# A two-layer graph network on one core: layer 1's values in one run, the transposes of x an iteration ahead, the output bias beside the scores

## The chip, the core and the metric

The kernel runs on one core of a Trainium2 chip. The core has engines with a queue each, which run side by side [...]: TensorE (PE, matmuls; PEld is its loading of weights), VectorE (DVE), ScalarE (ACT), GpSimd (POOL), and SyncE, whose queue (SPq) issues the DMAs. The metric is device time in microseconds (us) from the first to the last instruction; the median of three runs counts.

## The reference

64 graphs of 256 nodes with 512 features go through two layers. Everything is fp32.

```python
# layer 0: graph attention, 8 heads of 64
feats = einsum('bnf,hfu->bhnu', X, W)
dense = leaky_relu(e_self[..., :, None] + e_neigh[..., None, :], 0.2)
att = softmax(dense + NEG_BIG * (1.0 - A))
x = layernorm(x + relu(einsum('bhij,bhju->bhiu', att, feats) + b))
# layer 1: attention plus adjacency and exp(-distance), both from the same matrix
qkv = x @ W_qkv
attn = 0.33 * softmax(q k^T * scale) + 0.33 * adj + 0.33 * exp(-adj)
x = layernorm(x + (attn v) @ W_out + b_out)
```

## The kernel before

**Tiling.** A graph's 256 nodes are two tiles of 128 rows. A large product (features of layer 0, q and k, v) is cut 2 by 2 by 2 and done with seven block products instead of eight (`seven`, L289). They are named p1 to p7 and are called here f-products (`pf_p`, features of layer 0), q-products (`pq_p`) and v-products (`pv_p`). Each adds up in one of three PSUM banks: p1, then p6, p7 and p4 in the bank "chain"; p2 in "alone"; p5, then p3 in "pair". A product of the chain is copied out by ACT (L309) before the next one may add to that bank, since the copy is of the partial sum. DVE then adds a bank to what was copied (L312, steps 11, 22, 12); step 22 reads "pair" after p5 and before p3, so p3 must wait for it.

**Transposes.** The seven products need x transposed, and sums of its quarters. x is loaded in blocks (`load`, L125, tile `xb`), turned by one DVE instruction (L121, tile `xT`), and four DVE subtractions make the sums (`left_factors`, L273, tile `xC`). The same is done with layer 0's output (`hb`, `hT`, `hC`). `xT` and `hT` share two buffers in turn.

**Three graphs at once.** An iteration b of the main loop (L1299) works on attention of layer 0 for graph b, on the projections and scores of layer 1 for graph b-1, on the attention of layer 1 for graph b-2, and on the features of layer 0 for graph b+1. It has two parts. `attention0_beside_projections1` (L1132): q-products, the weights of layer 0 (`weights`, L632, tiles `pT`, four buffers for eight heads), their product with the features (`product` of attend0, L648), v-products, norm of layer 0, f-products. `attention1_beside_projections0` (L1212): values of layer 1 (L903), scores (L798), output projection (L991), the softmax's sums, `hT`. 

**What sets the order.** Each engine's order is written out by hand: `do` (L1030) calls one step, and `in_order` (L86) ties every instruction to the one before it on its engine, so no engine overtakes within its own queue. An instruction that waits holds everything behind it on that engine. The values of layer 0 come in two halves of four heads; "product g, t" is half g for node tile t. Half 1 reuses the four `pT` buffers of half 0.

**The long transfer.** Layer 0's row factors go from PE (`pr`) through ACT and DVE to HBM and back to all partitions (`gs`, then `gb`, 1 MB; L482 to 487). DVE's `nd` (L528) waits for `gb`, then ACT makes `ccol` (L535), then DVE makes `pT` (L637).

**Norm of layer 0.** DVE's `end` (L681) adds x and the row sums, POOL makes the mean (L346), ACT squares two tiles and reads two accumulators (L351), POOL makes the factors, ACT scales (L367). Then layer 0's output goes to HBM and comes back in blocks as `hb`.

Of the kernel before, what the change touches and what calls it, by code (L numbers as in the profile page):

```python
# [8 lines left out]
FT = mybir.dt.float32  # L9
# [8 lines left out]
def kernel(  # L18
# [30 lines left out]
    P = 128  # L49
    NB, N, F = x.shape  # L50
    H, _, U = w0.shape
    T = N // P
    C = F // P
# [326 lines left out]
    def attention_vectors(g, step):  # L380
# [30 lines left out]
                )  # L411
        in_order()

    def proj0(b):
        xT = work.tile([P, C, N], FT, tag="xT", name=f"xT_{b}")
        if b > 1:
            xC = work.tile([P, 4, C2, P], FT, tag="xC", name=f"xC_{b}", bufs=1)

        V0[b] = work.tile([P, T, H, UX], FT, tag="v0", name=f"v0_{b}", bufs=1)
        if b > 1:  # L420
# [178 lines left out]
                    scale=V0[b][:, t, h, U : U + 1],  # L599
                )  # L600

        def transposes():
            transpose_blocks(xT, XB[b])
            if b > 1:
                left_factors(xC, xT)

        return dict(
            copied=copied,
            logits=logits,
            maxima=maxima,  # L610
            factors=factors,
            xT=transposes,
            product=product,
            add=add,
            bias=bias,
# [267 lines left out]
    def attend1(b):  # L883
# [139 lines left out]


    stages = dict(
        proj0=proj0, attend0=attend0, proj1=proj1, softmax1=softmax1, attend1=attend1
    )
    S = {}

# [8 lines left out]
    def start():  # L1038

        tiles = [slice(t, t + 1) for t in range(T)]  # L1040
        do("proj0", 0, "xT_rows")
        for g in range(2):
            for t in range(T):
                do("proj0", 0, "features", t, g)
                do("proj0", 0, "logits", t, g)
                do("proj0", 0, "copied", t, g)
            if g == 0:
                do("proj0", 0, "aT")
                load_adj(1)
                do("proj0", 0, "far")  # L1050
        attention_vectors(0, 0)
        attention_vectors(1, 0)
        do("proj0", 0, "maxima")
        attention_vectors(0, 1)
        do("proj0", 1, "xT")
        do("proj0", 0, "columns")
        do("proj0", 0, "factors")
        attention_vectors(1, 1)
        attention_vectors(0, 2)
        attention_vectors(1, 2)  # L1060
        attention_vectors(2, 0)
        attention_vectors(3, 0)
        for h in range(2):
            do("proj0", 0, "scaled", h)
            do("attend0", 0, "weights", h)
        attention_vectors(2, 1)
        attention_vectors(3, 1)
        attention_vectors(2, 2)
        attention_vectors(3, 2)
        for h in range(2, HG):  # L1070
            do("proj0", 0, "scaled", h)
            do("attend0", 0, "weights", h)
        do("proj0", 1, "features", 0, 0)
        do("proj0", 1, "features", 0, 1)
        do("attend0", 0, "product", 0, 0)
        do("attend0", 0, "product", 0, 1)
        for h in range(HG, H):
            do("proj0", 0, "scaled", h)
            do("attend0", 0, "weights", h)
        do("proj0", 1, "features", 1, 0)  # L1080
        do("attend0", 0, "product", 1, 0)
        do("attend0", 0, "product", 1, 1)
        do("proj0", 1, "features", 1, 1)
        do("attend0", 0, "norm0", 0, 0)
        do("attend0", 0, "norm0", 0, 1)
        combine_weights1(0)
        do("attend0", 0, "norm0", 1, 0)
        do("attend0", 0, "end", tiles[0])
        do("attend0", 0, "squares", tiles[0])
        do("attend0", 0, "norm0", 1, 1)  # L1090
        do("attend0", 0, "end", tiles[1])
        do("attend0", 0, "squares", tiles[1])
        do("attend0", 0, "norm", tiles[0])
        for t in range(T):
            for g in range(2):
                do("proj0", 1, "copied", t, g)
        load_rows(1)
        do("proj0", 1, "maxima")
        do("proj0", 1, "columns")
        do("proj0", 0, "shared")  # L1100
        do("proj0", 1, "aT")
        do("proj1", 0, "from_rows", 0)
        do("attend0", 0, "norm", tiles[1])
        do("proj1", 0, "qk", "p1")
        do("proj1", 0, "from_rows", 1)
        do("proj1", 0, "hC")
        do("proj1", 0, "qk", "p2")
        do("proj0", 1, "far")
        do("proj0", 1, "factors")
        combine_weights1(1)  # L1110
        combine_weights1(2)
        load(2)
        load_adj(2)
        do("proj1", 0, "qk_add", 11)
        do("proj1", 0, "qk", "p6")
        for h in range(HG):
            do("proj0", 1, "scaled", h)
            do("attend0", 1, "weights", h)
        do("proj1", 0, "qk", "p5")
        do("proj1", 0, "qk", "p7")  # L1120
        do("proj1", 0, "qk_add", 22)
        combine_weights1(3)
        for h in range(HG, H):
            do("proj0", 1, "scaled", h)
            do("attend0", 1, "weights", h)
        do("proj1", 0, "qk", "p4")
        do("proj1", 0, "qk", "p3")
        do("proj1", 0, "qk_add", 12)
        right_factors(wf_sb, wf12)
        in_order()  # L1130

    def attention0_beside_projections1(b):  # L1132


        if b > 1:
            do("attend1", b - 3, "squares")
            do("proj1", b - 1, "qk", "p1")
            do("proj1", b - 1, "qk", "p2")
            do("proj0", b, "columns")
            do("proj1", b - 1, "qk", "p6")  # L1140
            for h in range(HG):
                do("proj0", b, "scaled", h)
                do("attend0", b, "weights", h)
            do("attend1", b - 3, "store")
            do("proj1", b - 1, "qk_add", 11)
            do("proj1", b - 1, "qk", "p5")
            do("proj1", b - 1, "qk", "p7")
            do("attend1", b - 2, "residual")
            do("proj1", b - 1, "qk_add", 22)
        do("attend0", b, "product", 0, 0)  # L1150
        if b > 1:
            for h in range(HG, H):
                do("proj0", b, "scaled", h)
            do("proj1", b - 1, "qk", "p4")
        do("attend0", b, "product", 0, 1)
        do("attend1", b - 2, "weights", 0)
        if b > 1:
            for h in range(HG, H):
                do("attend0", b, "weights", h)
        do("attend0", b, "norm0", 0, 0)  # L1160
        do("attend0", b, "norm0", 0, 1)
        if b > 1:
            do("proj1", b - 1, "qk", "p3")
            do("proj1", b - 1, "qk_add", 12)
        do("proj0", b + 1, "xT")
        if b == 1:
            do("proj0", 1, "shared")
            load_rowmask()
            nc.sync.dma_start(bo_bc, b_out.partition_broadcast(P))
            nc.sync.dma_start(wo_sb, w_out.rearrange("(c p) f -> p c f", p=P))  # L1170
            in_order()
        if b + 2 < NB:
            load(b + 2)
        do("proj1", b - 1, "values", "p1")
        do("proj1", b - 1, "values", "p2")
        do("proj1", b - 1, "v_add", 11)
        do("attend0", b, "product", 1, 0)
        do("proj1", b - 1, "values", "p6")
        do("proj1", b - 1, "values", "p5")
        do("attend0", b, "product", 1, 1)  # L1180
        do("attend1", b - 2, "weights", 1)
        do("attend0", b, "norm0", 1, 0)
        do("attend0", b, "norm0", 1, 1)
        do("attend0", b, "end")
        do("proj1", b - 1, "values", "p7")
        do("proj1", b - 1, "v_add", 22)
        do("proj0", b + 1, "product", "p1")
        do("proj1", b - 1, "values", "p4")
        do("proj0", b + 1, "product", "p6")
        do("proj1", b - 1, "values", "p3")  # L1190
        do("attend0", b, "squares")
        do("attend1", b - 2, "weights", 2)
        do("proj1", b - 1, "v_add", 12)
        do("proj0", b + 1, "product", "p5")
# [17 lines left out]
    def attention1_beside_projections0(b):  # L1212


        do("attend1", b - 2, "values", 0)
        do("attend1", b - 2, "values", 1)
        do("softmax1", b - 1, "scores", 0)
        do("proj0", b + 1, "shared")
        do("softmax1", b - 1, "both", 0)
        do("softmax1", b - 1, "scores", 1)  # L1220
        do("softmax1", b - 1, "both", 1)
        do("proj0", b + 1, "bias")
        do("attend1", b - 2, "values", 2)
        do("attend1", b - 2, "values", 3)
        do("softmax1", b - 1, "scores", 2)
        do("softmax1", b - 1, "both", 2)
        do("softmax1", b - 1, "scores", 3)
        do("softmax1", b - 1, "both", 3)
        do("attend1", b - 2, "project", 0)
        do("proj0", b + 1, "rows")  # L1230
        do("proj1", b, "hT")
        do("attend1", b - 2, "project", 1)
        do("softmax1", b - 1, "sums")
        do("softmax1", b - 1, "invert")
        ps_tile([P, F], f"turn_{b}")

    def end():
# [113 lines left out]
```

## Time and profile before

| | |
|---|---|
| time, median of three | 3157.45 us (3157.37 to 3158.32) |
| busy: PE, PEld | 3032.9 us (96%), 2329.3 us (74%) |
| busy: DVE, ACT, POOL | 2628.4 us (83%), 1492.4 us (47%), 202.1 us (6%) |
| DMA | 328.20 MB, mean 104 GB/s |
| granted TensorE clock | 0.99 |
| chain that ended last | PE 53%, DVE 33%, ACT 7%, DMA 5% |

A timeline of the profile has one row for each run of equal instructions: start in us, duration in us, engine, source line, operation, output<-inputs, shape and count. What stands in brackets at its end is how long the engine was idle before it and which engine's instruction ended that. The duration of a row reaches to the end of its last instruction; the next row can begin a little earlier, because instructions of one engine overlap, so distances between starts ("pitch") are what adds up. One iteration is the distance between two equal rows: `pv_p` after its wait stands at 2022.63 us and again at 2070.74, 2118.56, 2166.38 and 2214.20, so 47.8 us (48.1 in the first of these).

### The profile page before, as it was taken

To read this page: it belongs to the slowest core of one execution; us is meant where nothing else is said; L and a number is where in the kernel's file an instruction comes from. 1 tells how busy PE (TensorE), PEld (TensorE's weight loads), DVE (VectorE), ACT (ScalarE), POOL (GpSimd) and SP (SyncE) were. 2 spreads that over 40 slices of the span, in tenths; PEclk is the share of its full clock that TensorE was granted. 3 is DMA by queue.
4 is the path that set the end of the run, shared out by engine and by line. 5 is a ranking of instruction groups with operands and counts; after the bars stand their busy time and mean duration, and the time that the engine had idled before them with its cause. 6 is when DMAs were issued, how large, how long until landed. Compare 5 with 4: busy or idle time off the path is not lost.

```text
span 3157.0 us, 64599 instructions
## 1 busy us (share of the span) xinstructions
PE 3032.9 (96%) x25526; PEld 2329.3 (74%) x25526; DVE 2628.4 (83%) x5151; ACT 1492.4 (47%) x3585; POOL 202.1 (6%) x526
## 2 busy tenths in 40 slices
PE   8899999999999999999999999999999999999998
PEld 7777777777777777777777777777777777777775
DVE  4888888888888888888888888888888888888885
ACT  2444444454454445444444544544444445445443
POOL 0000000000000000000000000000000000000000
PEclk7999999999999999999999999999999999999999
DMA  5344344344344344443444444444434434444331
GB/s 122 77 112 107 99 115 103 98 122 95 105 121 96 106 107 99 112 107 97 117 95 105 123 93 108 109 98 111 107 98 116 98 102 122 95 105 115 94 97 47
DMA packets 760611, 328.20 MB, mean 104 GB/s; under 512 B 693516, under 2 KB 694268, under 8 KB 744312
## 3 DMA queue, kind: packets, MB, share of 16 engines
q1 hardware_dynamic: 758200, 323.55, 40.6%
q8 instruction: 204, 3.34, 0.5%
q14 instruction: 95, 0.78, 0.1%
q10 hardware_dynamic: 2112, 0.52, 0.1%
HBM read 256.13 MB, written 67.61 MB: 103 GB/s over the span
## 4 chain that ended last, share of the span: by engine, by line
PE 53%; DVE 33%; ACT 7%; DMA 5%; issue 2%; SPq 0%; POOL 0%; DVEq 0%; POOLq 0%
PE po L994 13%; PE pq_p L300 9%; PE pf_p L300 9%; PE pz L804 8%; PE av L909 7%; DVE pT L637 7%; DVE p L899 5%; DVE p L892 4%; PE pv_p L300 3%; ACT v L595 3%; DVE qk L312 3%; DVE x L686 3%; DVE x L675 3%; DMA gb<-gs 2%; DVE xT L121 2%
## 5 line engine op out<-in xcount | busy, mean ns | idle before, releaser
L300 PE MATMUL pq_p<-hC,wqk_sb 128*128 128x128 f32 x4096 | 487.3, 277 | 4.2 <-ACT qk L309 4.2
L300 PEld LDWEIGHTS pq_p<-hC,wqk_sb 128*128 128x128 f32 x4096 | 469.1, 192 | 10.4 <-ACT qk L309 5.7
L994 PE MATMUL po<-wo_sb,oT 128*128 128x512 f32 x1024 | 466.3, 599 | 0.0
L637 DVE SCALAR_TENSOR_TENSOR pT<-gb,ccol,at 128x256 f32<-128x256 f32 x992 | 403.4, 479 | 17.6 <-ACT ccol L535 17.6
L300 PE MATMUL pq_p<-hT,wqk_sb 128*128 128x128 f32 x3072 | 380.9, 281 | 3.5 <-DVE hT L121 2.5
L300 PEld LDWEIGHTS pq_p<-hT,wqk_sb 128*128 128x128 f32 x3072 | 356.6, 193 | 34.3 <-DVE hC L278 23.9
L309 ACT COPY v<-pv_p 128x256 f32<-128x256 f32 x256 | 95.4, 373 | 573.5 <-PE pv_p L300 573.3
L300 PE MATMUL pv_p<-wv_sb,hC 128*128 128x256 f32 x1024 | 274.0, 400 | 95.5 <-DVE v L312 95.5
L351 ACT ACTIVATE junk<-x,nmean_l 128x512 bf16<-128x512 f32 x256 | 184.8, 722 | 342.9 <-POOL nmean_l L346 338.8
L813 ACT ACTIVATE p<-pz,hide 128x512 f32<-128x512 f32 x512 | 310.3, 689 | 59.6 <-PE pz L804 59.5
L994 PEld LDWEIGHTS po<-wo_sb,oT 128*128 128x128 f32 x1024 | 184.7, 190 | 207.5 <-issue 206.1
L899 DVE TENSOR_TENSOR p<-p,ct 128x1024 f32<-128x1024 f32 x252 | 308.7, 1225 | 8.6
L892 DVE TENSOR_TENSOR p<-p,rb 128x1024 f32<-128x1024 f32 x252 | 304.4, 1208 | 7.8 <-DMA rb<-rs 7.8
L660 PEld LDWEIGHTS av<-v,pT 128*64 128x64 f32 x8192 | 259.4, 138 | 57.5 <-issue 21.6
L660 PE MATMUL av<-v,pT 128*64 128x65 f32 x8192 | 294.5, 225 | 0.0
L300 PEld LDWEIGHTS pv_p<-wv_sb,hC 128*128 128x128 f32 x1024 | 179.3, 190 | 147.8 <-DVE v L312 121.7
L825 DVE SCALAR_TENSOR_TENSOR both<-p 128x512 f32<-128x512 f32 x256 | 176.6, 690 | 99.2 <-ACT p L813 99.1
L595 ACT ACTIVATE v<-v 128x64 f32<-128x64 f32 x1024 | 258.5, 339 | 0.0
L300 PE MATMUL pf_p<-wf_sb,xC 128*128 128x264 f32 x992 | 258.1, 394 | 0.0
L804 PE MATMUL pz<-qk 64*128 64x256 f32 x2048 | 256.2, 389 | 0.8 <-ACT p L813 0.8
L909 PE MATMUL av<-p,v 128*64 128x256 f32 x2016 | 245.4, 385 | 0.0
L804 PEld LDWEIGHTS pz<-qk 64*128 64x128 f32 x2048 | 187.1, 186 | 67.9 <-ACT p L813 26.0
(137 smaller groups left out, 3797.2 us busy)
## 6 DMA issues: line engine op xcount, KB each, us to landing
rb<-rs SPq DMA_DIRECT2D x63, 1024.0 KB, 4.7
gb<-gs SPq DMA_DIRECT2D x62, 1028.0 KB
xb<-in_x_dram SPq DMA_DIRECT2D x252, 128.0 KB, 3.7
x<-in_x_dram SPq DMA_DIRECT2D x63, 512.0 KB
hs<-x SPq DMA_DIRECT2D x63, 512.0 KB
hb<-hs SPq DMA_DIRECT2D x252, 128.0 KB, 3.5
out_dram<-x SPq DMA_DIRECT2D x63, 512.0 KB, 3.9
adj<-in_adj_dram SPq DMA_DIRECT2D x256, 64.0 KB, 4.4
```

The lines of the kernel that those rows point to most:

```text
L300: matmul(d, lhsT, rhs, start=(p in FIRST and i == 0), stop=(i == len(todo) - 1), skip_group_check=True,)
L351: nc.scalar.activation(junk, self.src[:, t, :], AF.Square, bias=self.nmean[:, t : t + 1], accum_out=self.rstd[:, t : t + 1],)
L595: nc.scalar.activation(V0[b][:, t, h, :U], V0[b][:, t, h, :U], AF.Copy, scale=V0[b][:, t, h, U : U + 1],)
L637: nc.vector.scalar_tensor_tensor(pT[h][:, j, :], GB[b][h], CCOL[b][:, j, h : h + 1], AT[b][:, j, :], op0=ALU.max, op1=ALU.mult,)
L660: matmul(av[r * half : (r + 1) * half, k, :], pT[h][:, j, i : i + half], V0[b][:, j, h, :UA], start=(j == 0), stop=(j == T - 1),)
L804: matmul(pz[:, r, j, :], QK[b][rows, g, 1, j * P : (j + 1) * P], QK[b][rows, g, 0, :], start=True, stop=True,)
L813: nc.scalar.activation(p[:, :, j, :], pz[:, :, j, :], AF.Exp, bias=hide[:, j, b : b + 1], scale=U**-0.5,)
L825: nc.vector.scalar_tensor_tensor(both[g], p[:, :, 0, :], TINY, p[:, :, 1, :], op0=ALU.add, op1=ALU.add)
L892: nc.vector.tensor_mul(p, p, REC[b][:, k : k + 2, g // 2, :] .unsqueeze(2) .to_broadcast([P, 2, T, N]),)
L899: nc.vector.tensor_add(p, p, CT[b].unsqueeze(1).to_broadcast([P, 2, T, N]))
L909: matmul(av[0][r * U : (r + 1) * U, g % 2, :], V1[b][:, j, 2 * g + r, :], PROBS[b][g][:, r, j, :], start=(j == 0), stop=(j == T - 1),)
L994: matmul(po, oT[:, c, t * P : (t + 1) * P], wo_sb[:, c, :], start=(c == 0), stop=(c == C - 1),)
```

## The change

Four moves; no instruction is added or left out.

1. **Layer 0's values in two visits.** PE did product 0,0; q p4; product 0,1; q p3; v p1, p2; product 1,0; v p6, p5; product 1,1; v p7. It now does product 0,0 and 0,1 together, q p4, q p3, product 1,0 and 1,1 together, and then v p1, p2, p6, p5, p7. DVE makes the second half's `pT` before the first `weights` of layer 1 and not after it, and `end` ahead of v's step 11 and layer 1's second `weights`.
2. **x's transposes an iteration ahead.** A new stage `turned` holds them. `xT` of graph b+2 is made in the second part of iteration b, after the bias of layer 0 and before the third `both` (L825); the four subtractions come at the end of the iteration, after `invert`. Before, both stood in the first part of iteration b+1, between q's step 12 and v's step 11.
3. **The output bias** (`residual`, L986) moves from between q's steps 11 and 22 to the scores, ahead of the projection.
4. **The norm of layer 0 ahead.** `squares` moves from after v p3 to after v p7, ahead of f p1. On ACT its two squares now stand between the copy of v p7 and the copy of f p1; before they stood after the copy of f p6.

```diff
+    def turned(b):
+        def transposes():
+            XT[b] = work.tile([P, C, N], FT, tag="xT", name=f"xT_{b}")
+            transpose_blocks(XT[b], XB[b])
+        def sums():
+            XC[b] = work.tile([P, 4, C2, P], FT, tag="xC", name=f"xC_{b}", bufs=1)
+            left_factors(XC[b], XT[b])
...
             do("proj1", b - 1, "qk", "p7")
-            do("attend1", b - 2, "residual")
             do("proj1", b - 1, "qk_add", 22)
         do("attend0", b, "product", 0, 0)
+        do("attend0", b, "product", 0, 1)
         if b > 1:
             for h in range(HG, H):
                 do("proj0", b, "scaled", h)
             do("proj1", b - 1, "qk", "p4")
-        do("attend0", b, "product", 0, 1)
-        do("attend1", b - 2, "weights", 0)
-        if b > 1:
             for h in range(HG, H):
                 do("attend0", b, "weights", h)
         do("attend0", b, "norm0", 0, 0)
         do("attend0", b, "norm0", 0, 1)
+        do("attend1", b - 2, "weights", 0)
         if b > 1:
             do("proj1", b - 1, "qk", "p3")
             do("proj1", b - 1, "qk_add", 12)
-        do("proj0", b + 1, "xT")
...
+        do("attend0", b, "product", 1, 0)
+        do("attend0", b, "product", 1, 1)
         do("proj1", b - 1, "values", "p1")
         do("proj1", b - 1, "values", "p2")
-        do("proj1", b - 1, "v_add", 11)
-        do("attend0", b, "product", 1, 0)
-        do("proj1", b - 1, "values", "p6")
-        do("proj1", b - 1, "values", "p5")
-        do("attend0", b, "product", 1, 1)
-        do("attend1", b - 2, "weights", 1)
         do("attend0", b, "norm0", 1, 0)
         do("attend0", b, "norm0", 1, 1)
         do("attend0", b, "end")
+        do("proj1", b - 1, "v_add", 11)
+        do("proj1", b - 1, "values", "p6")
+        do("proj1", b - 1, "values", "p5")
+        do("attend1", b - 2, "weights", 1)
         do("proj1", b - 1, "values", "p7")
         do("proj1", b - 1, "v_add", 22)
+        do("attend0", b, "squares")
         do("proj0", b + 1, "product", "p1")
         do("proj1", b - 1, "values", "p4")
         do("proj0", b + 1, "product", "p6")
         do("proj1", b - 1, "values", "p3")
-        do("attend0", b, "squares")
         do("attend1", b - 2, "weights", 2)
...
         do("proj0", b + 1, "bias")
+        if b + 2 < NB:
+            do("turned", b + 2, "xT")
...
         do("softmax1", b - 1, "both", 3)
+        do("attend1", b - 2, "residual")
         do("attend1", b - 2, "project", 0)
...
         do("softmax1", b - 1, "invert")
+        if b + 2 < NB:
+            do("turned", b + 2, "xC")
```

More of the change, by code (lines that the diff above doesn't have):

```diff
@@ L412, in attention_vectors @@
         in_order()
+    XT, XC = {}, {}
+    def turned(b):
[5 more added lines that the diff above has]
+            left_factors(XC[b], XT[b])
+        return dict(xT=transposes, xC=sums)
     def proj0(b):
-        xT = work.tile([P, C, N], FT, tag="xT", name=f"xT_{b}")
-        if b > 1:
-            xC = work.tile([P, 4, C2, P], FT, tag="xC", name=f"xC_{b}", bufs=1)
+        if b == 0:
+            XT[b] = work.tile([P, C, N], FT, tag="xT", name=f"xT_{b}")
+        xT, xC = XT[b], XC.get(b)
         V0[b] = work.tile([P, T, H, UX], FT, tag="v0", name=f"v0_{b}", bufs=1)
@@ L600, in scaled @@
                 )
[L602 to L605, printed above, removed]
         return dict(
@@ L611, in proj0 @@
             factors=factors,
-            xT=transposes,
             product=product,
@@ L1025 @@
     stages = dict(
-        proj0=proj0, attend0=attend0, proj1=proj1, softmax1=softmax1, attend1=attend1
+        turned=turned, proj0=proj0, attend0=attend0, proj1=proj1, softmax1=softmax1, attend1=attend1
     )
@@ L1054, in start @@
         attention_vectors(0, 1)
-        do("proj0", 1, "xT")
+        do("turned", 1, "xT")
         do("proj0", 0, "columns")
@@ L1154, in attention0_beside_projections1 @@
             do("proj1", b - 1, "qk", "p4")
-        do("attend0", b, "product", 0, 1)
-        do("attend1", b - 2, "weights", 0)
-        if b > 1:
             for h in range(HG, H):
@@ L1164, in attention0_beside_projections1 @@
             do("proj1", b - 1, "qk_add", 12)
-        do("proj0", b + 1, "xT")
-        if b == 1:
-            do("proj0", 1, "shared")
+        else:
+            do("turned", b + 1, "xT")
+            do("turned", b + 1, "xC")
+            do("proj0", b, "shared")
             load_rowmask()
```

## The prediction

> **What bounds the kernel now.** I read the page first, then the waits, then the timelines of PE, DVE and ACT over one ordinary iteration. The page has PE busy nearly all the time, so only what PE still waits for can be won.
>
> ```profile
> PE 3032.9 (96%) x25526; PEld 2329.3 (74%) x25526; DVE 2628.4 (83%) x5151; ACT 1492.4 (47%) x3585; POOL 202.1 (6%) x526
> ```
>
> The waits of PE come down to one: a v-product waits for a DVE addition, 63 times, that is once per iteration. (Columns: engine and line, whom it waited for, us in total, times, longest.)
>
> ```profile
> PEld pv_p L300 <- DVE v L312: 121.7, 63, 3.7
> PE pv_p L300 <- DVE v L312: 95.5, 63, 3.3
> ```
>
> PE's timeline shows where. The `pv_p` at 2022.63 is v p3, which stands idle until v's step 22 has read the bank "pair".
>
> ```profile
> 2017.49 1.13 PE L300 MATMUL pv_p<-wv_sb,hC 128*128 128x256 f32 x4
> 2018.46 1.05 PE L300 MATMUL pf_p<-wf_sb,xT 128*128 128x264 f32 x4
> 2019.35 1.03 PE L300 MATMUL pv_p<-wv_sb,hT 128*128 128x256 f32 x4
> 2020.21 1.05 PE L300 MATMUL pf_p<-wf_sb,xC 128*128 128x264 f32 x4
> 2022.63 1.13 PE L300 MATMUL pv_p<-wv_sb,hC 128*128 128x256 f32 x4 [1.36 <-DVE v L312]
> ...
> 2028.14 1.95 PE L909 MATMUL av<-p,v 128*64 128x256 f32 x16
> ```
>
> DVE's timeline says why. From `nd` to step 22 (2022.15) it hardly rests, and xT with xC lies in that stretch. Later, beside the scores, DVE idles several times.
>
> ```profile
> 2014.37 1.23 DVE L121 STREAM_TRANSPOSE xT<-xb 128x1024 f32<-128x1024 f32 x1
> 2015.63 0.42 DVE L276 TENSOR_TENSOR xC<-xT 128x256 f32<-128x256 f32 x1
> ...
> 2017.11 0.42 DVE L312 TENSOR_TENSOR v<-pv_p,v 128x256 f32<-128x256 f32 x1
> ...
> 2022.15 0.42 DVE L312 TENSOR_TENSOR v<-pv_p,v 128x256 f32<-128x256 f32 x1
> ...
> 2036.31 0.69 DVE L825 SCALAR_TENSOR_TENSOR both<-p 128x512 f32<-128x512 f32 x1 [0.79 <-ACT p L813]
> ...
> 2039.91 0.69 DVE L922 SCALAR_TENSOR_TENSOR x<-po,x 128x512 f32<-128x512 f32 x1 [1.75 <-PE pr L82]
> ...
> 2049.24 0.18 DVE L528 TENSOR_TENSOR nd<-v,gb 128x16 f32<-128x16 f32 x1 [1.58 <-DMA gb<-gs]
> ```
>
> ACT's timeline is where the change will bite: three copies, each right after its product, and then the two squares of layer 0's norm.
>
> ```profile
> 2018.66 0.37 ACT L309 COPY v<-pv_p 128x256 f32<-128x256 f32 x1 [2.63 <-PE pv_p L300]
> 2019.61 0.38 ACT L309 COPY v<-pf_p 128x264 f32<-128x264 f32 x1 [0.57 <-PE pf_p L300]
> ...
> 2021.31 0.38 ACT L309 COPY v<-pf_p 128x264 f32<-128x264 f32 x1 [0.52 <-PE pf_p L300]
> 2022.58 0.72 ACT L351 ACTIVATE junk<-x,nmean_l 128x512 bf16<-128x512 f32 x1 [0.89 <-POOL nmean_l L346]
> 2023.20 0.19 ACT L351 ACTIVATION_READ_ACCUMULATOR junk<-x,nmean_l 128x1 f32 x1
> 2023.42 0.72 ACT L351 ACTIVATE junk<-x,nmean_l 128x512 bf16<-128x512 f32 x1
> 2024.05 0.19 ACT L351 ACTIVATION_READ_ACCUMULATOR junk<-x,nmean_l 128x1 f32 x1
> ```
>
> [...]
> - [...] I therefore take starts, not durations, for PE.
> - [...]
> - [...] at 2027.54 an ACT copy of 0.36 us begins, and the next instruction starts at 2027.80, a pitch of 0.26. So I use pitches for what queues up, and ends for what another engine waits for.
>
> **The change, part by part.**
>
> *Transposes ahead.* xT and xC take DVE from 2014.37 to 2017.11, 2.74 us, out of the stretch before step 22. They go to the idle places. xT (pitch 1.26) enters the 0.79 before the third `both`, which starts 0.3 to 0.4 us later; before the fourth there are 0.47 us idle, so that one is on time again. The sums need 2015.63 to 2017.11 = 1.48 us of the 1.58 in which DVE waits for `gb`. Cost nothing; hidden by ACT's exponentials and the 1 MB transfer. Buffers stay in turn (xT, hT, xT), and `xb` is now free an iteration before it is loaded.
>
> *Bias.* L987 is 1.22 us (pitch 1.14) and goes into the 1.75 us before L922: nothing. What it frees is little: q's step 22 behind it waited for ACT's copy of q p7 anyway (ACT's copy runs 2005.90 to 2006.47, the step starts at 2006.50).
>
> *Two visits.* q p4 waited for the copy of q p7 in some iterations (4.2 us of PE in the whole run, 0.24 us in the iteration at 1524.75). Two products (pitch 1.08 each) now lie between, so it goes. The `pT` of heads 4 to 7 start after step 22 at 2007.11 and need the second product's first heads done (that product now starts at 2006.63, and a head takes 0.27): free. They are done 3.17 us later, 2010.3; PE wants them at 2005.55 + 2×1.08 + q p4 and p3, 1.98 + 1.89, = 2011.6. No wait. v p6 now follows v p2 directly and needs the copy of v p1: that copy starts 0.20 after p2 does and ends 0.37 later, under p2's 0.91. No wait.
>
> *DVE after all this.* Up to step 12 of q (2013.77) the work is the same in another order. Step 22 of v then comes 2.74 us earlier, 2019.41 to 2019.83. PE without waits wants v p3 at 2020.21 + 0.93 (a block's pitch is 0.87 to 0.97) = 2021.14. The wait goes with 1.3 us to spare. It is worth 2022.63 − 2021.14 = 1.49 us an iteration.
>
> *Squares ahead: the new wait.* `end` is now over at 2022.15 − 2.74 − 0.33 (step 11) − 2.39 (layer 1's weights) = 2016.7, POOL's mean at 2017.1. ACT reaches the squares only after the copy of v p7, at S + 0.20 + 0.26, with S = 2018.46 the start of f p1: 1.8 us after the mean. The squares hold ACT 1.57 us (in the layer 1 norm: first square 2045.66, next copy 2047.23). So the copy of f p1 starts at S + 2.03, ends 0.38 later, and f p6, which adds to that bank, starts 0.05 later: S + 2.46. Without the squares it starts at S + 1.75 (2020.21). PE is held **0.71 us** an iteration. Behind f p6 are v p3 and all of PE. Lower bound: zero, if PE has slipped that far for another reason. Upper: 0.71 plus what the mean is late beyond its 1.8 us of slack; I bound it at 1.5, for 0.8 of lateness.
>
> *Sum.* Removed: 95.5 of waits, less the 3.3 of the first iteration, whose xT stays, = 92; plus 61 × 0.13 (1.49 against 1.36) = 8; plus 4 at q p4: 104 us. Added: 61 × 0.71 = 43. Net −61: 3157.5 − 61 = **3096 us**.
>
> **The rivals.**
> - *The squares cost nothing* (all of the removed wait is won): 3157 − 104 = 3053. Against: the queue on ACT is in order and the arithmetic is short.
> - *Part of the old wait returns.* Layer 0's first multiply (L675) writes the buffer of the graph stored three iterations before. The store is issued at 2006.02 and lands after 2.8 to 5.0 us (median 3.9), 2008.8 to 2011.0. The multiply moves from 2012.88 to about 2010.5, so it can wait 0.5 us, and the `xb` load now comes right behind the store. Or xC makes `nd` late where `gb` is early (idle before it 1.10 us in one iteration). For: these slacks are thin. Against: v p3 has 1.3 us to spare, and 0.7 more since f p6 is held. If 1 us an iteration remains: 3096 + 61 × 0.5 to 1.0 = 3126 to 3157.
> - *Slower.* DVE's `end` comes 2.7 us late or more, the mean holds the squares, and ACT holds f p6 by over 1.7 us: 61 × 1.9 − 104 = +12, 3169. For: this wait chain crosses four engines, and all of PE hangs on it. Against: 1.8 us of slack.
>
> **How the numbers follow.** My forecast (3080 to 3110) has 0.62, the free squares 0.12, part of the wait back 0.17, slower 0.09. The likeliest gives 3096. The range takes in the lower bound of the squares' cost (3053) and half of the second rival: 3050 to 3126; about 0.17 is left out. Faster by over 0.2% (below 3151): 0.88; same: 0.03; slower: 0.09.
>
> **What would show it.** PE's waits must show `pf_p` waiting for ACT's `v` L309, some 0.6 to 0.8 us each, and no more 1.36 us before v p3. On ACT the two squares must stand between copies of v and start without waiting for POOL. DVE must idle some 2 us before f's step 22. The iteration must shrink from 47.8 to 46.9 or 47.0. I am wrong if L351 waits for the mean, if `nd` starts later after `gb` has landed, if L675 waits for a DMA, or if PE gains a wait outside f p6.

## The result and the profile after

| | before | after |
|---|---|---|
| time, median | 3157.41 us | 3048.72 us (3047.68 to 3049.53) |
| ratio | 1 | 0.9658, 95% interval 0.9641 to 0.9675 |
| ordinary iteration | 47.82 us | 46.31 us |

The change made the kernel 3.4% faster, 109 us. I had forecast 61 us and a range of 3050 to 3126, so the direction was right, and the time lies just below the range.

PE's share of busy time rises from 96% to 98%:

```profile
PE 2981.7 (98%) x25526; PEld 2325.0 (76%) x25526; DVE 2613.8 (86%) x5151; ACT 1472.8 (48%) x3585; POOL 278.6 (9%) x526
```

Among the waits of the kernel after, that of v p3 for DVE's step 22 is gone. In its place PE waits for ACT's copy (engine and line, whom it waited for, us in total, times, longest):

```profile
PEld pf_p L300 <- ACT v L309: 63.0, 62, 6.0
PE pf_p L300 <- ACT v L309: 38.1, 62, 5.6
DVE x L684 <- DMA out_dram<-x: 10.7, 22, 1.0
DVE nd L543 <- DMA gb<-gs: 7.9, 10, 2.2
```

PE's timeline of one iteration after:

```profile
2028.17 2.09 PE L669 MATMUL av<-v,pT 128*64 128x65 f32 x64
2030.19 2.05 PE L300 MATMUL pq_p<-hC,wqk_sb 128*128 128x128 f32 x16
2032.08 1.95 PE L300 MATMUL pq_p<-hT,wqk_sb 128*128 128x128 f32 x16
2033.96 2.09 PE L669 MATMUL av<-v,pT 128*64 128x65 f32 x64
2035.97 1.99 PE L300 MATMUL pv_p<-wv_sb,hT 128*128 128x256 f32 x8
2037.80 2.75 PE L300 MATMUL pv_p<-wv_sb,hC 128*128 128x256 f32 x12
2040.39 1.05 PE L300 MATMUL pf_p<-wf_sb,xT 128*128 128x264 f32 x4
2041.28 1.03 PE L300 MATMUL pv_p<-wv_sb,hT 128*128 128x256 f32 x4
2042.84 1.16 PE L300 MATMUL pf_p<-wf_sb,xC 128*128 128x264 f32 x4 [0.53 <-ACT v L309]
...
2049.24 1.95 PE L918 MATMUL av<-p,v 128*64 128x256 f32 x16
```

The row at 2042.84 is f p6. It starts 2.45 us after f p1 (2040.39); the prediction said 2.46. Its bracket has only 0.53 us of the 0.70 us lost, because idle time counts from the end of the row before (1.03 us after its start), and without a wait the next row starts 0.86 us after it. ACT's timeline shows the cause: the squares stand between two copies, and the first of them starts without a wait for the mean.

```profile
2040.59 0.37 ACT L309 COPY v<-pv_p 128x256 f32<-128x256 f32 x1 [1.35 <-PE pv_p L300]
2040.86 0.72 ACT L351 ACTIVATE junk<-x,nmean_l 128x512 bf16<-128x512 f32 x1
...
2042.43 0.36 ACT L309 COPY v<-pf_p 128x264 f32<-128x264 f32 x1
```

What the prediction did not have stands in the upper half of PE's timeline. From the first product of layer 0 to f p1 it is 2040.39 − 2028.17 = 12.22 us. Before it was 2018.46 − 2005.55 = 12.91 us, with the same matmuls and no wait in either. The difference of 0.69 us is hidden inside rows that count as busy. Rows of the kernel before that the prediction does not show:

```profile
2005.55 1.15 PE L660 MATMUL av<-v,pT 128*64 128x65 f32 x32
2006.63 2.05 PE L300 MATMUL pq_p<-hC,wqk_sb 128*128 128x128 f32 x16
2008.61 1.15 PE L660 MATMUL av<-v,pT 128*64 128x65 f32 x32
...
2023.60 1.94 PE L300 MATMUL pf_p<-wf_sb,xC 128*128 128x264 f32 x8
...
2044.25 3.84 PE L300 MATMUL pq_p<-hT,wqk_sb 128*128 128x128 f32 x32
2047.93 5.55 PE L300 MATMUL pq_p<-hC,wqk_sb 128*128 128x128 f32 x48
```

With the prediction's 1.49 us for the wait of v p3, an ordinary iteration adds up to 1.49 − 0.70 (f p6 held) + 0.69 (order on PE) = 1.48, against a measured 47.82 − 46.31 = 1.51. The kernel before also had late iterations, which the kernel after has not: 60 iterations from 145.51 to 3033.49 took 2887.98 us, 18.8 more than 60 × 47.82.

### The profile page after: what moved, and what is told of

It is laid out like the page before. It is cut to its first block, busy times and chain, and to the rows that moved or that the text cites. A ratio compares the mean times of both kernels' runs of the same rounds, so it can differ in the third digit from the quotient of the medians.

```text
span 3047.2 us, 64666 instructions
## 1 busy us (share of the span) xinstructions
PE 2981.7 (98%) x25526; PEld 2325.0 (76%) x25526; DVE 2613.8 (86%) x5151; ACT 1472.8 (48%) x3585; POOL 278.6 (9%) x526
## 4 chain that ended last, share of the span: by engine, by line
PE 74%; DVE 12%; ACT 9%; issue 3%; DMA 1%; SPq 0%; POOL 0%; DVEq 0%; POOLq 0%; ACTq 0%
PE pq_p L300 19%; PE po L1003 15%; PE pf_p L300 11%; PE pz L813 8%; PE av L918 8%; PE pv_p L300 6%; PE av L669 4%; ACT junk L351 3%; DVE pT L646 3%; DVE p L901 3%; ACT v L610 2%; PE pd L842 2%; ACT x L367 2%; DVE x L684 2%; DVE p L908 1%
## 5 line engine op out<-in xcount | busy, mean ns | idle before, releaser
L300 PE MATMUL pq_p<-hT,wqk_sb 128*128 128x128 f32 x3072 | 374.6, 279 | 3.2 <-DVE hT L121 1.9
L669 PE MATMUL av<-v,pT 128*64 128x65 f32 x8192 | 267.0, 223 | 0.6 <-DVE pT L646 0.6
L669 PEld LDWEIGHTS av<-v,pT 128*64 128x64 f32 x8192 | 249.3, 138 | 16.5 <-issue 1.4
L300 PEld LDWEIGHTS pf_p<-wf_sb,xC 128*128 128x128 f32 x992 | 184.7, 191 | 91.0 <-ACT v L309 63.0
L346 POOL TENSOR_SCALAR nmean_l<-sums_l 128x2 f32<-128x2 f32 (+1 forms) x130 | 28.4, 219 | 2453.4 <-DVE x L931 1321.2
L300 PE MATMUL pv_p<-wv_sb,hC 128*128 128x256 f32 x1024 | 243.3, 380 | 0.5 <-DVE v L312 0.5
```

Source lines behind the costliest of these rows:

```text
L300: matmul(d, lhsT, rhs, start=(p in FIRST and i == 0), stop=(i == len(todo) - 1), skip_group_check=True,)
L669: matmul(av[r * half : (r + 1) * half, k, :], pT[h][:, j, i : i + half], V0[b][:, j, h, :UA], start=(j == 0), stop=(j == T - 1),)
```

## The experiments

The kernel before took 3156.26 us beside the runs of the squares back, the four visits, the transposes back and the bias back, and 3155.28 us beside the other three. Each ratio is to it. A "visit" is a stretch in which PE does one kind of product with nothing else between; a "change" is a place where PE goes from matmuls of one weight shape to those of another.

### The squares back behind v p3 (move 4 undone)

```diff
         do("proj1", b - 1, "v_add", 22)
-        do("attend0", b, "squares")
         do("proj0", b + 1, "product", "p1")
...
         do("proj1", b - 1, "values", "p3")
+        do("attend0", b, "squares")
```

> The kernel after, with the squares of layer 0's norm put back behind v p3 (move 4 undone). Theory A: f p6 is held 0.70 us an iteration by the squares between the copies, so this gives back 61 x 0.70 = 43 us: 3006 us, iteration 45.6 us, no wait of f p6 in PE's waits. Up to 20 us of it may be lost where the later norm holds ACT's copies beside the scores. Theory B (the squares cost nothing because PE waits there for something else anyway): 3049 us, no change.

Measured: 2996.40 us, ratio 0.9496 (0.9471 to 0.9520). PE runs through without a wait:

```profile
2004.22 1.05 PE L300 MATMUL pf_p<-wf_sb,xT 128*128 128x264 f32 x4
2005.11 1.03 PE L300 MATMUL pv_p<-wv_sb,hT 128*128 128x256 f32 x4
2005.97 1.05 PE L300 MATMUL pf_p<-wf_sb,xC 128*128 128x264 f32 x4
2006.86 1.03 PE L300 MATMUL pv_p<-wv_sb,hC 128*128 128x256 f32 x4
```

Theory A holds: f p6 starts 1.75 us after f p1, and an ordinary iteration is 45.51 us. Move 4 costs 52 us where 43 were expected. Most of the rest is that f p6 after its wait also takes longer, 1.00 us to the next start against 0.89 here (61 × 0.11 = 7 us). So the free squares, a rival in the prediction whose time of 3053 lies close to the result, were not what happened.

### Layer 0's products in four visits again (moves 2 and 3 alone)

```diff
         do("attend0", b, "product", 0, 0)
-        do("attend0", b, "product", 0, 1)
...
             do("proj1", b - 1, "qk", "p4")
+        do("attend0", b, "product", 0, 1)
...
-        do("attend0", b, "product", 1, 0)
-        do("attend0", b, "product", 1, 1)
         do("proj1", b - 1, "values", "p1")
         do("proj1", b - 1, "values", "p2")
+        do("attend0", b, "product", 1, 0)
         do("proj1", b - 1, "values", "p6")
         do("proj1", b - 1, "values", "p5")
+        do("attend0", b, "product", 1, 1)
```

DVE's steps around them stand as before too, and the squares behind v p3.

> Moves 2 and 3 alone: as e1_squares_back, with layer 0's products again in four visits between q- and v-products (move 1 undone too). Theory A: each change between layer 0's products and the others costs PE time that the timeline's starts show and no wait shows; 0.70 us an iteration, so this is 61 x 0.70 = 43 us slower than e1_squares_back: 3049 us. Theory B (PE's order costs nothing; the extra gain came from DVE's slack against late transfers alone): equal to e1_squares_back within 5 us.

Measured: 3040.61 us, ratio 0.9637 (0.9616 to 0.9658), 44 us slower than with two visits. PE's timeline:

```profile
2021.81 1.15 PE L669 MATMUL av<-v,pT 128*64 128x65 f32 x32
2022.89 2.05 PE L300 MATMUL pq_p<-hC,wqk_sb 128*128 128x128 f32 x16
2024.87 1.15 PE L669 MATMUL av<-v,pT 128*64 128x65 f32 x32
2025.96 2.05 PE L300 MATMUL pq_p<-hT,wqk_sb 128*128 128x128 f32 x16
2027.85 1.89 PE L300 MATMUL pv_p<-wv_sb,hT 128*128 128x256 f32 x8
2029.67 1.15 PE L669 MATMUL av<-v,pT 128*64 128x65 f32 x32
2030.75 1.99 PE L300 MATMUL pv_p<-wv_sb,hC 128*128 128x256 f32 x8
2032.67 1.15 PE L669 MATMUL av<-v,pT 128*64 128x65 f32 x32
2033.76 1.13 PE L300 MATMUL pv_p<-wv_sb,hC 128*128 128x256 f32 x4
2034.72 1.05 PE L300 MATMUL pf_p<-wf_sb,xT 128*128 128x264 f32 x4
```

To f p1 it is 2034.72 − 2021.81 = 12.91 us, the same as before. No row has a wait. The price is seen by comparing starts with the kernel after: two visits of 32 matmuls take 1.08 us each, one of 64 takes 2.02, not 2.16. The q-product between two visits takes 1.98, and 1.89 with a visit at one side alone. v p6, p5 and p7 take 1.92 + 0.96 with a visit between, and 2.59 without. With two visits four of eight changes are gone, and those four cost 0.69 us, 0.17 each. A change between f- and v-products, which have the same shape of weights (128*128 in the row), costs nothing: they alternate at 0.86 to 0.89 us, and three v-products in a row take 2.59 / 3 = 0.86. What differs in the costly changes is the shape, 128*64 against 128*128. The products of layer 0 also have fewer columns (128x65), but the run with layer 1's values below removes a change between two kinds that both have 256, and it gains nearly the same, 0.15 us. The rows show how long a change takes, not what PE does meanwhile.

### One half in two visits

As the squares-back kernel, with product 1,0 and 1,1 apart again as in the diff above (and DVE's steps around them as before), and 0,0 and 0,1 together.

> As e1_squares_back, with the products of the second half of heads alone in two visits again (v p1, p2; product 1,0; v p6, p5; product 1,1; v p7). Theory A: half of the changes of kind come back. The starts in the timelines split the 0.70 us as 0.24 for the first half and 0.46 for the second, so 61 x 0.46 = 28 us: 3024 us; by the count of changes alone it would be 61 x 0.35 = 21 us: 3018 us. Theory B (what costs is not the change of kind but that the queues of DVE and ACT stand otherwise): nearer to 2996 or to 3041 than to these.

Measured: 3020.75 us, ratio 0.9564 (0.9549 to 0.9579), 24 us slower than with two visits (two changes more), 20 faster than with four. The time lies between the count of changes (21 expected) and my split by the starts (28). The trace decides for the count: an ordinary iteration is 45.86 us, in the middle of 45.51 (two visits) and 46.21 (four), and it is 12.57 us from the first product to f p1, in the middle of 12.22 and 12.91. PE has no wait in that stretch in any of the three. Theory A stands, and B falls.

### Layer 1's values in one visit

```diff
-        do("attend1", b - 2, "values", 0)
-        do("attend1", b - 2, "values", 1)
         do("softmax1", b - 1, "scores", 0)
...
+        do("attend1", b - 2, "values", 0)
+        do("attend1", b - 2, "values", 1)
         do("attend1", b - 2, "values", 2)
         do("attend1", b - 2, "values", 3)
         do("softmax1", b - 1, "scores", 2)
```

> As e1_squares_back (2996 us), and the four groups of layer 1's values in one visit between scores 1 and scores 2, where before they were two pairs, one ahead of scores 0. One change of kind less on PE per iteration. Theory A: a change of kind costs PE 0.17 us (0.70 us for the four that e2_four_visits has more), so 61 x 0.17 = 10 us: 2986 us. Theory B (only layer 0's products, with their 64 columns of weights, have such a cost, or ACT's exponentials, now in another order, hold the scores): 2996 us or more.

Measured: 2991.94 us (2987.31 to 2993.67), ratio 0.9476 (0.9459 to 0.9493), 4.5 us below the squares-back kernel (2995.92 to 2998.27). Its stretch from the last f-product to the projection:

```profile
2005.68 2.00 PE L813 MATMUL pz<-qk 64*128 64x256 f32 x16
2007.61 3.67 PE L918 MATMUL av<-p,v 128*64 128x256 f32 x32
2011.21 2.00 PE L813 MATMUL pz<-qk 64*128 64x256 f32 x16
2013.14 3.70 PE L1003 MATMUL po<-wo_sb,oT 128*128 128x512 f32 x8
```

It is 7.46 us long, and 7.61 in the squares-back kernel (2012.27 to 2019.88): 0.15 us for one change less, as theory A says, or 9 us in all. In the two profiled executions all of it arrived: the 61 iterations together are 9.0 us shorter. In the medians it is half; where the rest went in the other executions stays open. In some iterations v p3 waits for step 22 again (PE 4.8 us in all in both kernels, 3.1 of it in the first iteration), so PE has come close to DVE there. This is the fastest version found, 5.2% below the kernel before.

### Transposes back (move 2 undone)

```diff
         if b > 1:
             do("proj1", b - 1, "qk", "p3")
             do("proj1", b - 1, "qk_add", 12)
-        else:
+        if b + 1 < NB:
             do("turned", b + 1, "xT")
             do("turned", b + 1, "xC")
```

and without the two calls in the second part of the iteration.

> The kernel after, with xT and xC back behind q's step 12 (move 2 undone). Theory A: DVE is 2.74 us later at the end of layer 0; of this 1.2 us is slack, so the mean comes 1.5 us after ACT is ready for the squares, and f p6 waits that much longer: 3049 + 61 x 1.5 = 3141 us, with L351 waiting for POOL's mean some 1.5 us. Theory B (PE's fewer visits were the whole gain, the transposes not): 3049 to 3070 us.

Measured: 3177.61 us, ratio 1.0069 (1.0047 to 1.0091): slower than the kernel before, and 37 us above the 3141 expected. ACT and PE of one iteration:

```profile
2032.52 0.72 ACT L351 ACTIVATE junk<-x,nmean_l 128x512 bf16<-128x512 f32 x1 [1.61 <-POOL nmean_l L346]
```

```profile
2034.50 1.16 PE L300 MATMUL pf_p<-wf_sb,xC 128*128 128x264 f32 x4 [2.25 <-ACT v L309]
```

The mean is late by 1.61 us in this iteration and by 1.50 in an ordinary one (1.5 expected), the squares stand in the copies' way, and f p6 waits 2.25 us, ordinarily 2.13. An ordinary iteration is 47.91 us; 61 × (47.91 − 46.31) = 98 us make 3146. The other 31 us are in late iterations, as the next run shows them. So moves 1, 3 and 4 gain nothing without the transposes ahead.

### Two visits alone (move 1 alone)

The kernel before with move 1 of the diff in it, the order on PE and on DVE, and nothing else.

> Move 1 alone: the kernel before with layer 0's products in two visits, transposes, bias and squares in their old places. Theory A: PE's 0.70 us an iteration are real, but v p3 still waits for DVE's step 22, whose chain is as long as before, so the saving turns into a longer wait (about 2.1 us where it was 1.36): 3157 us within 8. Theory B (the saving counts by itself): 3157 - 43 = 3114 us.

Measured: 3168.36 us (3163.31 to 3174.66), ratio 1.0039 (1.0021 to 1.0056). PE's saving became a longer wait for the same DVE step:

```profile
2032.45 1.13 PE L300 MATMUL pv_p<-wv_sb,hC 128*128 128x256 f32 x4 [2.14 <-DVE v L312]
```

Ordinarily this wait is 2.04 us, and an ordinary iteration stays at 47.8 us. Theory A is right in that, but the run is 13 us above the kernel before: there are more late iterations, and the mean granted clock of the profiled execution is 0.987 where the kernel before has 0.990. What happens there is seen best in the kernel before. Its iteration at 1829.64 waited 2.00 us for step 22. The stretch after that wait (length; busy time of PE, PEld, DVE, ACT and POOL with their instructions; granted clock; DMA share; GB/s):

```profile
1829.64:1833.64 4.00, 4.00 (x11) 3.17 (x12) 2.63 (x3) 1.57 (x4) 1.60 (x3) 0.57 0.01 2
```

For 4 us the clock is at 0.57, and the next equal row comes 49.51 us later, 1.69 late. In the kernel with two visits alone two waits of 3.3 and 3.4 us were followed by 0.57 as well. Not every wait of 2 us does it (those at 722.48 and 1541.39 did not).

Between 140 us and the last 15 us, the records of the granted clock have four lowered stretches in the kernel before, which begin at 1106.24, 1444.16, 1829.87 and 2649.07, and none in the kernel after. Each is 3.41 us at a clock of 0.50, and from one start to the next it is 99, 113 and 240 times 3.413 us. Here are two neighbouring stretches of this grid around the wait at 722.48, and two around the one at 1829.64:

```profile
720.54:723.95 3.41, 1.47 (x7) 1.30 (x8) 3.38 (x8) 1.85 (x5) 0.22 (x1) 1.00 0.15 23
723.95:727.36 3.41, 3.41 (x17) 2.92 (x16) 2.68 (x6) 1.91 (x5) 1.60 (x3) 1.00 0.00 0
1826.46:1829.87 3.41, 1.41 (x7) 0.93 (x6) 3.34 (x11) 1.04 (x3) 0.22 (x1) 1.00 0.50 80
1829.87:1833.28 3.41, 3.41 (x9) 2.64 (x9) 2.40 (x3) 1.34 (x4) 1.60 (x3) 0.50 0.01 2
```

PE was busy for 1.41 us in the stretch before the lowered one, and for 1.47 us where the clock stayed. In the stretches before the four lowered ones it was busy for 1.42, 1.19, 1.41 and 1.42 us, and in each of the grid's other stretches in this run for at least 1.47 us.

With two visits alone PE's timeline has twelve iterations of this kind: from the start of v p3 to layer 1's values they take 7.19 or 7.20 us, the others 5.51 or 5.52. The length of the wait does not tell them apart: the stretch is 7.20 us long after a wait of 2.04 us (the row at 1935.01) and 5.51 after one of 3.40 us (the row at 142.60). Each of the twelve loses 1.69 us, and the 8 more than in the kernel before account for the 13 us of this run (8 × 1.69 = 14). With the transposes back the mean granted clock is 0.987 as well; how much of the 31 us there is the clock was not shown.

### The bias back (move 3 undone)

```diff
             do("proj1", b - 1, "qk", "p7")
+            do("attend1", b - 2, "residual")
             do("proj1", b - 1, "qk_add", 22)
...
-        do("attend1", b - 2, "residual")
         do("attend1", b - 2, "project", 0)
```

> The kernel after, with the output bias back between q's steps 11 and 22 (move 3 undone). Theory A: DVE waits 1.35 us for ACT's copy there, the addition takes 1.14 us and fits in: no change, 3049 us within 3. Theory B (the bias was on DVE's chain): 61 x 1.1 us less slack, slower by 10 us or more.

Measured: 3045.70 us (3043.86 to 3048.15), ratio 0.9653 (0.9631 to 0.9674). The times overlap with those of the kernel after (3047.68 to 3049.53), and an ordinary iteration is 46.31 us in both: the bias is free in both places.

## Why the prediction was right and wrong

The runs give the change as a sum of steps: moves 2 and 3 alone −116 us (3156 to 3041), move 1 on top −44 (to 2996), move 4 on top +52 (to 3049). Each figure holds in this order: move 1 alone, without move 2, gained nothing.

**The step that failed** is the part "Two visits". There I costed the order on PE by its waits alone: a wait at q p4 "goes", and "no wait" elsewhere. I carried the pitches of before, 1.08 us a product and 1.98 for q p4, over into the new order as if they were the instructions' own. They contained the cost of coming from another kind of matmul. The runs put 44 us there (0.69 us an iteration in the starts), in a term that the sum did not have. Of the 47 us between 3096 and 3049 that is nearly all; 12 us more won at the removed wait and 9 more lost to the squares almost cancel. It was to be had from the profile of before: the 1.98 us of the q-product between two products of layer 0 (2008.61 − 2006.63) stood beside (2047.93 − 2044.25) / 2 = 1.84 for two q-products in a row. The term also took from DVE's slack: of the 1.3 us that v p3 was to have to spare, the squares-back kernel has 0.6 (step 22 ends 2006.26, v p3 starts 2006.86).

**The removed wait** was right in kind and place. Its size: I had 104 us, and moves 2 and 3 brought 116. An ordinary iteration lost 1.61 us (47.82 to 46.21) and not 1.49, because v p3 after its wait takes 0.97 us to the next start (2022.63 to 2023.60), and 0.86 without one (2043.84 to 2044.70 in the kernel after); this makes 7 us. Another 7 or so are the lowered clock in four iterations of before (4 × 1.69 us); I counted their extra waiting, mostly for a late `gb`, but not the clock behind it. Both v p3 and f p6 add to the very sums that DVE or ACT still has to read, so they had to wait for those reads in any case.

**The squares ahead** were right to the hundredth in the start of f p6 (2.45 us after f p1, 2.46 predicted, mean in time). The cost was 52 us and not 43, for the most part by what f p6 loses after its wait. The lower bound of this cost, zero, is what gave the range its low end; the result lies near it by another way.

**Transposes** cost nothing where they went: in the kernel after DVE waited for `gb` only 7.9 us in all, and step 22 starts at 2042.03, well before v p3 at 2043.84. But the 1.58 us in which the sums were to fit came from an iteration with a late `gb`. In 49 of 62 iterations of before that idle time was under 1.48 us, mostly 1.1 to 1.3, so `nd` now follows xC at once and starts some 0.3 us later after `gb` has landed. The prediction named this as a sign of being wrong; it stayed inside v p3's slack.

**Rivals.** The wait for the store came as feared (L684, which is L675 of the kernel before, waits up to 1.0 us, 22 times) and stayed inside the slack. The mean held the squares only in the first iteration of the kernel after; with the transposes back it did, by 1.50 us in an ordinary iteration, and there the kernel was slower than before, as the third rival described.

## What to carry to other kernels

When PE changes its order, price the changes between weight shapes too, 0.17 us each here: no wait shows them, only the distances between starts, and one has to compare a kind in a long run with the same kind between others. A saving on one engine counts only if the engine that it waits for is given room as well: two visits alone made the kernel 0.4% slower, and with the transposes out of the way the same edit gave 44 us. And of a change in several moves, take the moves apart: here one of four cost 52 us, and without it the other three brought about half as much again as all four together (2996 us, against 3049 with all and 3157 before).

## What I had not expected of the hardware

- A change between matmuls with weights 128*64 and 128*128 cost PE about 0.17 us in this fp32 kernel, counted as busy time (12.91, 12.57 and 12.22 us with eight, six and four changes); f- and v-products with equal weight shape alternated free.
- A wait of PE of 2 us was in some iterations followed by half the clock for 3.41 us, at a loss of 1.69 us, and once a wait of 3.4 us was not. What told them apart in the kernel before was PE's busy time within one stretch of the 3.413 us grid: 1.42 us or less ahead of the four lowered stretches, against 1.47 or more elsewhere.
- POOL's two short steps of the norm took 0.69 and 0.71 us in the kernel before and 1.02 and 1.69 us in the kernel after, for the same 128x2 elements. In the kernel after, DVE's layer 1 weights (128x1024) run beside both; in the kernel before, only beside the first:

```profile
2042.61 1.02 POOL L359 TENSOR_SCALAR rstd_l<-rstd_l 128x2 f32<-128x2 f32 x1 [2.92 <-ACT junk L351]
2043.71 1.69 POOL L362 TENSOR_TENSOR rstd_l<-rstd_l,mhalf 128x2 f32<-128x2 f32 x1
```

The cause was not tried; the norm had the time.
